# Edge-gated graph layer: early stores on another queue with rows taken earlier, low parts copied across partitions, expansion placed behind the aggregation

## Chip, cores and metric

One core of one Trainium2 chip. The metric is device time of one execution in microseconds. Each kernel runs several times in rounds beside the kernel before on the same chip. Chips differ by over 1% (the kernel before has medians of 1219 to 1235 us in four comparisons, three of them on chips known to differ), so only ratios are compared across chips. All runs told of here gave a correct result. Two timed runs were in the slow state (one of the kernel before at 1242.29 us, one of b_early_expand at 1246.37 us); the ratios leave them out. All profiles are of fast runs.

## The reference

```python
# x: [16, 1024, 256]; A_a = A_m = adj: [1024, 1024], about 1% non-zero
pre_u = einsum('bud,dk->buk', h, W1[:d]);  pre_v = einsum('bvd,dk->bvk', h, W1[d:])
hidden = relu(pre_u[:, :, None, :] + pre_v[:, None, :, :] + b1)
S = sigmoid(einsum('buvk,ko->buvo', hidden, W2)[..., 0] + b2[0])
a = einsum('buv,bud->bvd', S * A_a, h)
m = einsum('uv,bud->bvd', A_m, h) * h
z = beta1 * h + beta2 * (a @ Wa + ba) + beta3 * (m @ Wm + bm)
```

## The kernel before

The kernel works on lists of edges. An opening makes a table with, for each node u, its `pre_u` row (a product on TensorE) and its `h` row, and the edge lists of the first 512 targets v. Then 320 steps follow, 10 to a block (a block is 128 targets times 4 batches). A step takes 128 edges:

- GpSimd gathers the edges' table rows into one of five buffers `fetched`;
- TensorE **expands** `pre_v` from targets to edges with a 0/1 matrix `mark` (`expand`, into one of two buffers `pc`);
- VectorE adds both and reduces relu times W2 (`gate`); ScalarE takes the sigmoid and scales the left side;
- one step later TensorE **aggregates** (`aggregate`).

In between run the products of the block: `pre_v` of the next block (`halves`), table rows, the output of the last block, and the remaining edge lists. All of these share two small buffers, `misc`, in PSUM, the memory that products are written to. A product's result is copied out of PSUM by ScalarE or VectorE; this is called its eviction here. `pre_v` is kept as a rounded high part and a low part, stacked on the two halves of the partitions, so that one fp32r product carries both. The low part is made on its own partitions and has to get to the other half.

```python
# lists(vt): stages of one edge list; the masks of a list go to all partitions
few = ...; nc.scalar.copy(few, mark)
yield
for w in range(NW):
    for h in range(2):
        nc.scalar.dma_start(whose[h * W:(h + 1) * W, vt * NW + w, :], few[w * W:(w + 1) * W])
pe = aside(vt)
...                                                   # 5 products into pe
nc.scalar.copy(L..., pe...)
yield                                                 # VectorE goes on from L
...
# halves(k): pre_v of block k
for h in range(2):
    step = yield
    p = small("p"); add_row(p, b1_p); half_product(p, hTs[order[k]], w_v, h, True)
    nc.scalar.copy(X[:, 0, c], p)
    after(step + 1, lambda: nc.vector.tensor_tensor(low[:, c], p, X[:, 0, c].bitcast(FP), ALU.subtract))
yield
nc.scalar.copy(X[W:, 1, :], X[W:, 0, :].bitcast(FP))
for h in range(2):
    yield
    pl = small("pl")
    nc.tensor.matmul(pl, swap, low[:, c], start=True, stop=True)
    for w in range(NW):
        s = slice((1 - w) * W, (2 - w) * W)
        nc.scalar.copy(X[s, w, c], pl[s])
...
# the opening: digits advance a list by a stage, r is half a table row tile, h a stage of halves(0),
# v the small gathers of list 0's values, f the first five gathers
script = ("r 0 0", "r r 0", "r 1", "0 r 1 1", "0 0 r r", "1 r 0 2 2", "r 0 0 v 2", "1 1 r r 2",
          "r 1 r 3 3", "1 1 2 2 r h", "2 r r h 3", "2 2 3 h", "3 3 f h h")
...
for n in range(total + 2):                            # k, s: block and step in it
    aggregate(n - 1); fetch_val(2); fetch(n - 1 + NF) # and half_end twice a block
    gate(n); left_adj(n + 1)
    ...                                               # load_mark twice a block
    do(n)                                             # work put off with after()
    ...                                               # lists, block_end, turn_over
    if k + 1 < BS and s in (0, 2, 3, 4, 7): ...       # halves(k + 1)
    ...                                               # table rows
    if n + 2 < total:
        expand(n + 2)
```

Order matters: every engine takes its instructions in the order of the program.

## Time and profile before

| | kernel before |
|---|---|
| median of 3 runs, us | 1236.83 (1234.14 to 1241.36) |
| span of the profiled execution, us | 1225.1 |
| busy us: TensorE, VectorE, ScalarE, GpSimd | 1110.8, 1068.5, 844.0, 416.3 |
| add's (L546) idle ahead of it, us | 68.9, of it 38.9 for the expansion |
| first gather, first add, first add of the second block, us | 68.62, 78.14, 131.3 |

The profiled execution took 1226.9 us, less than any of the timed runs. Busy shares over the span mix an opening with no full engine and a loop with three nearly full ones, so they must be read by stage. The prediction below shows those views. Two groups matter later (columns: busy us, mean ns | idle us of the engine just ahead, with what ended it):

```profile
L546 DVE TENSOR_TENSOR t<-fetched,pc 128x1024 f32<-128x1024 f32 x320 | 389.2, 1216 | 68.9 <-PE pc L530 38.9 <-DMA fetched<-table,uidx 11.5 <-PE misc L385 4.8
L420 DVE TENSOR_TENSOR low<-misc,X 128x512 fp32r<-128x512 f32 x64 | 44.0, 687 | 20.6 <-ACT X L419 20.2 <-issue 0.3
```

### The profile page before, as it was taken

The numbers are of one execution on the slowest core, as the hardware profiler recorded it, in microseconds if no ns is written. First come the engines' busy times: TensorE is split into PE (matmuls) and PEld (weight loads), VectorE is DVE, ScalarE is ACT, GpSimd is POOL, SyncE is SP. The second block draws the span as 40 slices with busy tenths as digits, with TensorE's granted clock in tenths as the row PEclk, the third lists the DMA queues.
The fourth block names the chain that finished last, engine by engine and source line by source line (L and its number), as shares of the span: only waits on it lengthen the run. The fifth ranks groups of instructions, "written<-read, shape, count | busy, mean of one in ns | idle before, by whom it ended". The sixth has DMA issues, their size and how long they took to land. (4 is left out here: it accounts for less than half of the span.)

```text
span 1225.1 us, 23939 instructions
## 1 busy us (share of the span) xinstructions
PE 1110.8 (91%) x7697; PEld 723.6 (59%) x7697; DVE 1068.5 (87%) x3517; ACT 844.0 (69%) x2562; POOL 416.3 (34%) x412
## 2 busy tenths in 40 slices
PE   7665989988888988999999999999999999999986
PEld 6543666645555655666666556666666655665553
DVE  7667868898997889899999999998888999999994
ACT  2245567766666756778777777777777777887763
POOL 0345562326244314423233333332222333333330
PEclk9777999989898989999999999999999999999998
DMA  9688899977889979899999999999998998999992
GB/s 285 221 296 296 268 321 330 335 262 237 315 291 332 353 295 343 323 356 362 356 363 375 351 355 325 347 351 394 387 358 322 353 322 315 329 339 329 325 334 97
DMA packets 151975, 393.50 MB, mean 321 GB/s; under 512 B 16816, under 2 KB 110512, under 8 KB 115632
## 3 DMA queue, kind: packets, MB, share of 16 engines
q0 software_dynamic: 49504, 299.85, 66.5%
q1 hardware_dynamic: 85776, 77.08, 19.5%
q10 hardware_dynamic: 16560, 14.95, 3.8%
q8 instruction: 63, 1.03, 0.3%
q14 instruction: 72, 0.59, 0.1%
HBM read 395.88 MB, written 50.33 MB: 364 GB/s over the span
## 5 line engine op out<-in xcount | busy, mean ns | idle before, releaser
L459 POOL DMA_INDIRECT fetched<-table,uidx x320 | 326.7, 1021 | 717.1 <-PE acc L567 525.5
L550 DVE SCALAR_TENSOR_TENSOR t<-t,w_b 128x256 f32<-128x256 f32 x1280 | 469.6, 422 | 19.8
L546 DVE TENSOR_TENSOR t<-fetched,pc 128x1024 f32<-128x1024 f32 x320 | 389.2, 1216 | 68.9 <-PE pc L530 38.9
L567 PE MATMUL acc<-fetched,left 128*32 128x256 f32 x4096 | 323.4, 393 | 28.1 <-ACT left L556 21.9
L556 ACT ACTIVATE left<-left,gt 128x32 f32<-128x32 f32 (+1 forms) x1280 | 300.3, 306 | 10.4
L530 PE MATMUL pc<-X,mark 128*128 128x512 f32 x640 | 249.8, 472 | 5.4 <-ACT mark L523 5.4
L567 PEld LDWEIGHTS acc<-fetched,left 128*32 128x32 f32 x4096 | 121.3, 110 | 195.6 <-issue 71.6
L553 ACT ACTIVATE gt<-sc,b_b 128x4 f32<-128x4 f32 x320 | 95.5, 299 | 158.8 <-DVE t L550 150.7
L385 PE MATMUL misc<-w_u,hT 128*128 128x256 f32 x512 | 132.7, 407 | 19.8 <-ACT fetched L401 8.4
L530 PEld LDWEIGHTS pc<-X,mark 128*128 128x128 f32 x640 | 120.0, 195 | 29.8 <-ACT mark L523 5.9
L615 PE MATMUL misc<-w_m,LT 128*128 128x256 f32 x496 | 133.7, 392 | 0.0
L615 PE MATMUL misc<-w_a,LT 128*128 128x256 f32 x496 | 127.3, 379 | 0.0
L385 PEld LDWEIGHTS misc<-w_u,hT 128*128 128x128 f32 x512 | 99.3, 203 | 43.9 <-ACT fetched L401 8.9
L385 PE MATMUL misc<-w_v,hT 128*128 128x256 f32 x512 | 122.6, 383 | 0.0
L540 ACT ACTIVATE left<-onehot,val 128x128 f32<-128x128 bf16 (+1 forms) x320 | 117.5, 367 | 0.0
L615 PEld LDWEIGHTS misc<-w_m,LT 128*128 128x128 f32 x496 | 88.9, 189 | 34.8 <-issue 25.5
L385 PEld LDWEIGHTS misc<-w_v,hT 128*128 128x128 f32 x512 | 98.3, 192 | 13.2
L343 POOL DMA_INDIRECT val<-in_adjT_dram,vidx x80 | 85.3, 1066 | 60.9 <-DVE b_p L194 33.4
L550 DVE DVE_READ_ACCUMULATOR t<-t,w_b 128x1 f32 x1280 | 104.0, 81 | 0.0
L575 ACT COPY ev<-acc 128x512 f32<-128x512 f32 x128 | 74.9, 585 | 41.6 <-PE acc L567 28.6
L615 PEld LDWEIGHTS misc<-w_a,LT 128*128 128x128 f32 x496 | 94.2, 190 | 12.8
L585 PE MATMUL misc<-ident,ev 128*128 128x128 f32 x512 | 81.0, 289 | 15.8 <-DVE h_blk L619 8.5
(140 smaller groups left out, 820.3 us busy)
## 6 DMA issues: line engine op xcount, KB each, us to landing
hT<-in_xT_dram SPq DMA_DIRECT2D x40, 512.0 KB
h_blk<-in_x_dram SPq DMA_DIRECT2D x31, 512.0 KB
out_dram<-h_blk SPq DMA_DIRECT2D x31, 512.0 KB
table<-tab SPq DMA_DIRECT2D x26, 512.0 KB
table<-in_x_dram ACTq DMA_DIRECT2D x24, 512.0 KB
fetched<-table,uidx POOLq DMA_INDIRECT x320
table<-in_x_dram SPq DMA_DIRECT2D x8, 512.0 KB
table<-fetched SPq DMA_DIRECT2D x6, 512.0 KB
```

Of the source, the lines that this page charges most:

```text
L343: nc.gpsimd.indirect_dma_start(out=val[:, i, j:j + 1], out_offset=None, in_=adj_flat, in_offset=bass.IndirectOffsetOnAxis(ap=vidx[:, i, j: ...
L385: nc.tensor.matmul(p[:, bb * D:(bb + 1) * D], hT[:, 2 * h + bb, i, :], wt[:, i, :], start=(i == 0 and not begun), stop=(i == DC - 1), skip ...
L459: nc.gpsimd.indirect_dma_start(out=fetched[n % NF], out_offset=None, in_=table[g], in_offset=bass.IndirectOffsetOnAxis(ap=uidx[:, vt * NW ...
L530: nc.tensor.matmul(pcs[n][:, c], marks[n // TW][:, j * P:(j + 1) * P], cuts[k][:, w, c], start=True, stop=True)
L540: nc.scalar.activation(lefts[n][:, :m, :, 0, :], onehot[:, i, o:o + m, :].unsqueeze(2).to_broadcast([P, m, GB, V]), AF.Copy, scale=val[:, ...
L546: nc.vector.tensor_tensor(t, fetched[n % NF][:, :GD].rearrange("p (b d) -> p b d", b=GB), pcs.pop(n).rearrange("p (b d) -> p b d", b=GB), ...
L550: nc.vector.scalar_tensor_tensor(t[:, b, :], t[:, b, :], 0.0, w2_b, ALU.max, ALU.mult, accum_out=sc[:, b:b + 1])
L553: nc.scalar.activation(gt, sc, AF.Sigmoid, bias=b2_b)
L556: nc.scalar.activation(lefts[n][:, :m, b, 1, :], lefts[n][:, :m, b, 0, :], AF.Copy, scale=gt[:, b:b + 1])
L567: nc.tensor.matmul(accs[h][b * 2 * V:(b + 1) * 2 * V, r, :], left[:, i, b].rearrange("p k v -> p (k v)"), f[:, GD + b * D:GD + (b + 1) * D ...
L585: nc.tensor.transpose(pt[:, i * P:(i + 1) * P], ev[:, r, c * P:(c + 1) * P], ident)
L615: nc.tensor.matmul(pz[:, bb * D:(bb + 1) * D], LTs[k][:, c, 2 * h + bb, i, :], wt[:, c, :], start=False, stop=(i == 1 and c == DC - 1), sk ...
```

## The change

Its intent: free ScalarE's queue in the opening, have the table's rows done sooner, take the swap off TensorE, and give VectorE its expansion before TensorE turns to the block's products. There are three parts. Part 1 is the copies, part 2 the place of the expansion, part 3 the opening (stores and script). `EARLY` is 4, so lists 0 to 3 are meant. The cut is shortened.

```diff
-    swap = fixed([P, P], "swap", FR)                     # and its two instructions
-                nc.scalar.dma_start(whose[...], few[...])
+                (nc.gpsimd if vt < EARLY else nc.scalar).dma_start(whose[...], few[...])
@@ halves
-        for h in range(2):
+        for w in range(NW):
             yield
-            c = slice(2 * h * D, (2 * h + 2) * D)
-            pl = small("pl")
-            nc.tensor.matmul(pl, swap, low[:, c], start=True, stop=True)
-            for w in range(NW):
-                s = slice((1 - w) * W, (2 - w) * W)
-                nc.scalar.copy(X[s, w, c], pl[s])
+            nc.scalar.copy(X[(1 - w) * W:(2 - w) * W, w, :], low[w * W:(w + 1) * W].bitcast(FP))
@@ script
-    "r 0 0", "r r 0", "r 1", "0 r 1 1", "0 0 r r", "1 r 0 2 2", "r 0 0 v 2", "1 1 r r 2",
-    "r 1 r 3 3", "1 1 2 2 r h", "2 r r h 3", "2 2 3 h", "3 3 f h h"
+    "r 0 0", "r r 0", "r 1", "0 r 1 1", "0 0 r r", "1 r 0 2 2", "r r 0 0 v 2", "1 1 r r",
+    "2 r 1 r", "2 2 r r 1 1 h", "2 h 3 3", "2 2 h 3", "f h h 3", "3 3"
@@ main loop
         do(n)
+        if n + 2 < total:
+            expand(n + 2)
         ...
-        if k + 1 < BS and s in (0, 2, 3, 4, 7):
+        if k + 1 < BS and s in (0, 2, 3, 4, 6):
         ...
-        if n + 2 < total:
-            expand(n + 2)
```

More of the change, by code (lines that the diff above doesn't have):

```diff
@@ L178 @@
         nc.vector.tensor_scalar(slot_of[:, w, :], upto[:, :TW], float(P), row, ALU.mult, ALU.add)
-    swap = fixed([P, P], "swap", FR)
-    for w in range(NW):
-        nc.vector.tensor_scalar(swap[:, w * W:(w + 1) * W], upto[:, (1 - w) * W:(2 - w) * W], row, None, ALU.is_equal)
     ident = fixed([P, P], "ident")
@@ L305, in lists @@
             for h in range(2):
-                nc.scalar.dma_start(whose[h * W:(h + 1) * W, vt * NW + w, :], few[w * W:(w + 1) * W])
+                (nc.gpsimd if vt < EARLY else nc.scalar).dma_start(whose[h * W:(h + 1) * W, vt * NW + w, :], few[w * W:(w + 1) * W])
         pe = aside(vt)
@@ L423, in halves @@
         nc.scalar.copy(X[W:, 1, :], X[W:, 0, :].bitcast(FP))
-        for h in range(2):
+        for w in range(NW):
             yield
-            c = slice(2 * h * D, (2 * h + 2) * D)
-            pl = small("pl")
-            nc.tensor.matmul(pl, swap, low[:, c], start=True, stop=True)
-            for w in range(NW):
-                s = slice((1 - w) * W, (2 - w) * W)
-                nc.scalar.copy(X[s, w, c], pl[s])
+            nc.scalar.copy(X[(1 - w) * W:(2 - w) * W, w, :], low[w * W:(w + 1) * W].bitcast(FP))
     engines = mybir.EngineType
@@ L477 @@
         copy_h(turn[i], nc.sync)
-    script = ("r 0 0", "r r 0", "r 1", "0 r 1 1", "0 0 r r", "1 r 0 2 2", "r 0 0 v 2", "1 1 r r 2",
-              "r 1 r 3 3", "1 1 2 2 r h", "2 r r h 3", "2 2 3 h", "3 3 f h h")
+    script = ("r 0 0", "r r 0", "r 1", "0 r 1 1", "0 0 r r", "1 r 0 2 2", "r r 0 0 v 2", "1 1 r r",
+              "2 r 1 r", "2 2 r r 1 1 h", "2 h 3 3", "2 2 h 3", "f h h 3", "3 3")
     m = 0
```

## The prediction

> **What bounds the kernel now.** I read the row of tenths first, to see which engines are full where.
>
> ```profile
> PE   7665989988888988999999999999999999999986
> ...
> DVE  7667868898997889899999999998888999999994
> ...
> PEclk9777999989898989999999999999999999999998
> DMA  9688899977889979899999999999998998999992
> ```
>
> Three stages. The first three slices (about 78 us of 1225) have no engine full: an opening made of waits. Up to slice 16 (about 500 us) TensorE and VectorE share the work with gaps. From there on TensorE, VectorE and DMA all read 9. The table by stretches (us, then busy us and counts of PE, PEld, DVE, ACT, POOL, then clock, DMA share, GB/s) tells the last stage apart:
>
> ```profile
> 78.10:150.00 71.90, 55.65 (x330) 37.33 (x330) 55.63 (x189) 36.65 (x109) 38.28 (x37) 0.83 0.88 297
> 150.00:300.00 150.00, 137.09 (x911) 89.28 (x909) 126.64 (x419) 101.09 (x305) 61.66 (x61) 0.95 0.87 300
> 300.00:500.00 200.00, 176.79 (x1199) 112.35 (x1201) 175.88 (x584) 133.63 (x410) 77.66 (x76) 0.95 0.89 313
> 500.00:700.00 200.00, 195.56 (x1431) 127.28 (x1423) 186.62 (x599) 156.85 (x483) 63.17 (x63) 1.00 0.98 364
> ```
>
> From 500 us TensorE is busy 195.56 of 200 us (98%) and VectorE 186.62 (93%): TensorE is the bound, VectorE 5% behind. In 150 to 500 us TensorE has 36 us of gaps in 350. The chain that ended last covers only the final 22 us, so it says nothing here. The timeline of one late step shows the order on TensorE:
>
> ```profile
> 905.40 1.07 PE L567 MATMUL acc<-fetched,left 128*32 128x256 f32 x16
> 905.51 1.22 DVE L546 TENSOR_TENSOR t<-fetched,pc 128x1024 f32<-128x1024 f32 x1
> ...
> 908.05 0.58 PE L428 MATMUL misc<-low,swap 128*128 128x512 f32 x1
> ...
> 908.47 0.63 PE L530 MATMUL pc<-X,mark 128*128 128x512 f32 x2
> ...
> 909.13 1.22 DVE L546 TENSOR_TENSOR t<-fetched,pc 128x1024 f32<-128x1024 f32 x1
> ```
>
> A step on TensorE is aggregation (L567), products of the block, swap, expansion (L530). VectorE's add (L546) takes the expansion finished just before it. The swap holds TensorE for 908.47 - 908.05 = 0.42 us.
>
> For the opening I read the timeline from 27 us:
>
> ```profile
> 27.35 4.94 ACTq L306 DMA_DIRECT2D whose<-few  x4
> ...
> 32.34 0.40 ACT L313 COPY L<-pc 128x290 f32<-128x290 f32 x1 [4.46 <-PE misc L385]
> ...
> 32.77 0.18 DVE L317 TENSOR_TENSOR s_of<-slot_of,L 128x10 f32<-128x10 f32 x1 [5.35 <-ACT L L313]
> ...
> 34.31 3.53 PE L385 MATMUL misc<-w_u,hT 128*128 128x256 f32 x8 [2.48 <-ACT fetched L401]
> ```
>
> Four issues of list 0's stores sit on ScalarE's queue for 4.94 us. The copy behind them comes that late, and VectorE and TensorE wait for it. Whom the trace names as releaser of the copy (a matmul long over) is not the cause; the queue is. The same happens to list 1 (47.30, 2.64 us; VectorE idle 4.83) and list 3 (81.24 to 84.04). Nothing else is full then: DMA moves only 142 GB/s from 40 to 65 us. The first gather goes out at 68.62, when the last row of the table has landed, and the first add starts at 78.14.
>
> **What the Trainium skill says.** "DMA: Bandwidth & Descriptors", Issuing engines are not separate DMA queues: starting DMAs from another engine saves only the issuing sequencer's time. Agrees in kind: an issue of these stores has a median of 0.608 us on ScalarE, and that time is what the change moves. "PSUM — Partial Sum Buffer", Engine vs sequencer instructions: ScalarE, VectorE and GpSimd are strict FIFOs and matmuls go in program order. Agrees: the copy at 32.34. So order is worth time here. "TensorE: Matmul & The Clock Gate", Back-to-back issue gap: N/2.4 + 2.5 ns warm, 216 ns for 512 columns. The trace has 0.42 us for a swap, about twice; the trace decides. "ScalarE: Activation LUTs", What ACT_TABLE_LOAD costs: 186 ns + 0.833 ns per element with immediates, so 612 and 1039 ns for 512 and 1024 columns. The trace has 581 and 1045.
>
> **Part 1, low parts without TensorE.** Gone per block: two swaps on TensorE and four copies of 64x512 from PSUM on ScalarE. New: two copies of 64x1024 in SBUF across partitions. Their duration is that of the form already there (L423):
>
> ```profile
> L431 ACT CAST X<-misc 64x512 fp32r<-64x512 f32 x128 | 74.4, 581 | 24.7 <-PE misc L428 20.2 <-PE acc L567 0.8
> L428 PE MATMUL misc<-low,swap 128*128 128x512 f32 x64 | 36.4, 569 | 23.1 <-ACT LT L588 11.6 <-issue 6.8 <-DVE from L280 3.1
> L423 ACT CAST X<-X 64x1024 fp32r<-64x1024 f32 x32 | 33.4, 1045 | 0.4
> ```
>
> ScalarE: 128 x 0.581 = 74.4 us become 64 x 1.045 = 66.9, so 7.5 us less; ScalarE is at 78% late, so this is worth little by itself. TensorE: 64 x 0.42 = 27 us of occupation go, 42 of the 64 after 500 us (17.6 us) and 20 between 78 and 500 (8.4 us). The waits around them go as well. Swap on the buffer from ScalarE (LT L588) and the next product on ScalarE's eviction (X L431) make 5.7 + 4.9 us plus 1.4 of small ones after 500, and about 5.3 + 2.3 + 5.9 + 0.5 = 14 between 150 and 500. Some of the latter waits will reappear at the next instruction, as they are ScalarE's or VectorE's lateness and not the swap's. Sum on TensorE: 17.6 + 12.0 = 29.6 late, 22 early.
>
> **Part 2, expansion right behind the aggregation.** Nothing is added or removed. The expansion comes 0 to 2 us earlier, ahead of the block's products. It needs a buffer that the add two steps back frees: for the expansion at 908.47 that is the add at 902.65, done at 903.87, while its new place is behind the aggregation's 16 issues, about 906.4. So TensorE doesn't stall for it in a TensorE-bound step. VectorE's waits for it should mostly go (L546 on pc L530: 38.9 us in all, 12.8 of them in 150 to 500 and 13.2 after 500). As VectorE isn't the bound, this pays only by letting it run ahead of steps in which it has more work. I choose 5 us over the whole loop, an estimate from the 7.4 + 9.0 us that TensorE waits for the gated left side (L556), of which a third may go.
>
> **What part 1 is worth in time.** After 500 us VectorE has 650 us of work in 700. Taking 29.6 us away gives 670, VectorE at 97% and the DMA at 349 x 700/670 = 365 GB/s on average. Two engines both near full don't reach that; I take 60%: 18 us. In 78 to 500 I take half of 22: 11 us.
>
> **Part 3, the opening.** Stores of lists 0 to 3 move to GpSimd, which idles until 35.97 us. List 0 then gives back about 4.4 us (28.4 in place of 32.8 for the copy's reader), list 1 about 2.6, and the third and fourth some 2 together. Two rows come before list 2's matters, and list 3 moves two script lines later. That takes VectorE work of 1.2 + 1.65 us (L246, L253) away from in front of list 1, and should take part of TensorE's 3.7 us waits for an eviction. On the other side GpSimd gets about eight issues at 0.6 us, with 0.3 us gaps, between the ten small gathers (36 to 50 us) and the first large gather: by an estimate from the L240 issues of 0.58 to 0.65 us, 7 us, ending at about 54 us if the small gathers start 4 us earlier. So the first large gather can't come before 54 and may come at 56 to 58 in place of 68.6. The burst behind it (400 GB/s from 75 to 100 us) moves along but isn't shortened. I take 10 us.
>
> **Sum.** 18 + 11 + 5 + 10 = 44 us; I take off 5 us for what several estimates in a row leave out: 39. 1236.8 - 39 = 1198.
>
> **Rivals.**
> (a) VectorE or ScalarE becomes the bound. For: VectorE is at 95% after 1000 us, and the new copies wait on VectorE's low parts. Against: these are made a step or more before the copy's turn. Then part 1 gives a third, 10 + 5, and the total is about 1212.
> (b) DMA is already the bound after 500 us, its share being 0.98. For: VectorE waits 10.1 us there for gathers. Against: that is 13 times in some 190 steps, and stretches of 25 us reach 393 to 408 GB/s. Then the late 18 us shrink to 5 and the total is about 1211.
> (c) GpSimd's queue delays the first gathers, its stores waiting for ScalarE's masks in front of gathers. For: strict order. Against: it has idle time up to 36 us. Then the opening gives nothing: about 1208.
> (d) The expansion waits for the add and holds up the block's products. For: in VectorE-late steps the add starts only when the aggregation does. Against: the aggregation itself lasts 0.6 to 1.0 us of the add's 1.22. It costs up to 0.3 us in a third of 320 steps: 30 us, which would eat most of the gain and give about 1225.
>
> **Range and chances.** One of (a) to (c) gives 1208 to 1212, at the limit of 2% (1212.1); all parts in full, with the opening at 15 us, give about 1182. So 1183 to 1215. Faster by over 2%: 0.74; within 2%: 0.24; slower: 0.02, as no work is added to a full engine.
>
> **What would show it.** Right: no swap row; TensorE busy about 27 to 30 us less at the same clock or better; 64 more copies of 64x1024 at about 1.04 us; L546's wait on pc under 15 us; first gather near 57 and first add near 67 us; the list copy L313 within 1 us of its matmuls. Wrong: the stretches from 500 us as long as before with L546 waiting on gathers (rival b), L530 waiting on VectorE's L546 for over 20 us (d), or the first gather still at 65 or later with GpSimd's stores just ahead of it (c).

## The result and the profile after

Median 1201.80 us (1200.57 to 1209.87, 4 runs) against 1235.49 us (1232.73 to 1241.36, 4 runs). The ratio of the fast runs is 0.9737, 95% interval 0.9689 to 0.9785. A ratio here is the mean time of one kernel's fast runs over that of the other's of the same rounds, so not quite the ratio of the medians. The kernel is faster. Two later comparisons, on two chips, gave 0.9757 and 0.9758.

The profiled execution (span 1208.1 us) is the longest of the four, while that of the kernel before was a short one, so the two profiles are only 17.0 us apart and not 33. Near 840 us TensorE waited 8.7 us for one load of transposed rows there. In another execution (the run after_third below) the same row product waits 4.1 us, put down there to an add long over. The block that holds this product (21, counted from 0) takes from 34.5 to 46.3 us in the fourteen traces (37.7 before, 46.0 after), without a pattern by part, so one execution's total moves by up to 12 us with it. Where it matters I therefore compare by block and not by the end.

The row of tenths of the kernel after:

```profile
PE   7767899897789888999999999997999999999986
...
DVE  7769878997989997999999999996789999999994
...
PEclk9878999899989999999999999998999999999998
DMA  9998999878989987999999999999899999999992
```

The pit at slice 28 (TensorE 7, VectorE 6) is the load just told of. The table by stretches, with the columns of the prediction's:

```profile
78.00:150.00 72.00, 59.76 (x384) 38.78 (x383) 61.97 (x214) 42.33 (x122) 47.34 (x45) 0.95 0.93 301
150.00:300.00 150.00, 133.60 (x925) 87.66 (x925) 126.66 (x412) 103.18 (x307) 59.66 (x59) 0.97 0.86 301
300.00:500.00 200.00, 176.33 (x1214) 114.69 (x1210) 179.41 (x605) 135.10 (x405) 75.26 (x74) 0.97 0.91 323
500.00:700.00 200.00, 197.78 (x1441) 129.87 (x1440) 190.78 (x608) 159.51 (x485) 64.88 (x64) 1.00 0.98 365
```

From 500 us TensorE is fuller than before (197.78 of 200), although its swaps are gone, and VectorE is at 190.78. Both were brought closer to full; neither has 5% to spare.

The opening, from the timeline of the kernel after (start and length in us, engine, line, operation; in brackets the engine's idle time just ahead and what ended it, where `issue` means that the profile shows no wait):

```profile
24.80 2.10 POOL L303 DMA_DIRECT2D whose<-few  x4 [22.22 <-ACT few L297]
...
28.14 0.40 ACT L310 COPY L<-pc 128x290 f32<-128x290 f32 x1 [0.47 <-PE pc L306]
...
28.57 0.17 DVE L314 TENSOR_TENSOR s_of<-slot_of,L 128x10 f32<-128x10 f32 x1 [1.36 <-ACT L L310]
...
55.56 1.07 POOL L451 DMA_INDIRECT fetched<-table,uidx  x1 [4.63 <-DMA table<-tab]
...
66.92 0.72 ACT L297 CAST few<-made 128x640 uint8<-128x640 f32 x1 [7.02 <-DVE made L291]
67.55 0.72 ACT L515 CAST mark<-whose 128x640 fp32r<-128x640 uint8 x1
...
69.59 1.22 DVE L538 TENSOR_TENSOR t<-fetched,pc 128x1024 f32<-128x1024 f32 x1 [2.04 <-PE pc L522]
```

The four stores of list 0 take 2.10 us on GpSimd, beside everything else (in the other traces with ScalarE's stores, they hold ScalarE's queue for 2.89, 3.09 and 6.36 us, so the 4.94 us before is not a fixed cost). ScalarE's copy follows its products at once (28.14 in place of 32.34), and VectorE idles 1.36 in place of 5.35 us. The first gather is 13 us earlier. The first add is only 8.5 us earlier: its mask (67.55) stands on ScalarE behind a copy for list 3, which waited 7.02 us for VectorE.

The groups that answer to those of before:

```profile
L538 DVE TENSOR_TENSOR t<-fetched,pc 128x1024 f32<-128x1024 f32 x320 | 388.8, 1215 | 22.0 <-DMA fetched<-table,uidx 8.2 <-PE pc L522 3.2 <-PE misc L577 1.1
L522 PE MATMUL pc<-X,mark 128*128 128x512 f32 x640 | 237.3, 453 | 23.6 <-DVE t L538 17.4 <-ACT mark L515 5.0 <-issue 1.2
L417 DVE TENSOR_TENSOR low<-misc,X 128x512 fp32r<-128x512 f32 x64 | 43.9, 686 | 48.6 <-ACT X L416 46.9 <-issue 1.7
L423 ACT CAST X<-low 64x1024 fp32r<-64x1024 f32 x64 | 66.8, 1044 | 0.8
```

The add no longer waits for the expansion (3.2 in place of 38.9 us). In its place VectorE waits for the high part of `pre_v` (46.9 in place of 20.2 us, of which 12.2 belong to the late load), and TensorE's expansion waits 17.4 us for the add that frees its buffer.

Where the time went, from the times of the first add of a block (us): before 78.1, at block 1 131.3, at block 11 524.2; after 69.6, 114.7 and 506.6. So the lead is 8.5 us at the loop's start, 16.6 one block later and 17.6 at block 11. The last can't be trusted: in the changed kernel's two later traces block 11 starts at 508.5 and 491.5 us. From block 11 to 19 the median block takes 31.83 against 32.53 us, from 24 to 30 it takes 31.10 against 31.53.

The 8 us won inside block 0 are mostly one step. In the kernel before the add of step 9 came 12.9 us after that of step 8:

```profile
117.96 0.59 ACT L588 COPY LT<-misc 128x512 f32<-128x512 f32 x1 [2.54 <-remote]
118.60 1.11 PE L585 MATMUL misc<-ident,ev 128*128 128x128 f32 x4 [4.28 <-issue]
...
120.39 0.80 PE L428 MATMUL misc<-low,swap 128*128 128x512 f32 x1 [0.68 <-ACT LT L588]
...
122.45 3.78 PE L385 MATMUL misc<-w_u,hT 128*128 128x256 f32 x8 [1.26 <-ACT X L431]
...
126.77 1.22 DVE L546 TENSOR_TENSOR t<-fetched,pc 128x1024 f32<-128x1024 f32 x1 [5.71 <-PE pc L530]
```

At 112.77 us a small product for list 4 had taken one of the two `misc` buffers, and VectorE read it at 129.46 only. So transposes, swap and row product queue for the one that is left, each behind ScalarE's eviction of the last, and the expansion stands behind them all. Not all of the step is this queue: the first eviction (117.96) waited 2.54 us for something that the profile doesn't name (`remote`), b_opening and b_early_expand have 3.76 and 4.30 us of the same there, and the changed kernel has none on record (1.01 us in after_again). The same place in the kernel after:

```profile
103.80 0.73 PE L522 MATMUL pc<-X,mark 128*128 128x512 f32 x2 [0.95 <-issue]
...
107.62 1.12 PE L577 MATMUL misc<-ident,ev 128*128 128x128 f32 x4 [1.81 <-ACT left L532]
...
109.41 3.56 PE L382 MATMUL misc<-w_u,hT 128*128 128x256 f32 x8 [0.68 <-ACT LT L580]
...
110.00 1.21 DVE L538 TENSOR_TENSOR t<-fetched,pc 128x1024 f32<-128x1024 f32 x1
```

The queue is still there but shorter, and the expansion came ahead of it, so the add takes place beside it: 4.5 us for the step.

### The profile page after: what moved, and what is told of

It is laid out like the page before. It is cut to its first block, busy times and chain, and to the rows that moved or that the text cites. A ratio compares the mean times of both kernels' runs of the same rounds, so it can differ in the third digit from the quotient of the medians.

```text
span 1208.1 us, 23816 instructions
## 1 busy us (share of the span) xinstructions
PE 1095.2 (91%) x7633; PEld 721.5 (60%) x7633; DVE 1066.6 (88%) x3515; ACT 838.6 (69%) x2498; POOL 424.3 (35%) x428
## 5 line engine op out<-in xcount | busy, mean ns | idle before, releaser
L559 PE MATMUL acc<-fetched,left 128*32 128x256 f32 x4096 | 333.3, 394 | 36.9 <-ACT left L548 20.5
L522 PE MATMUL pc<-X,mark 128*128 128x512 f32 x640 | 237.3, 453 | 23.6 <-DVE t L538 17.4
L559 PEld LDWEIGHTS acc<-fetched,left 128*32 128x32 f32 x4096 | 128.7, 110 | 184.9 <-issue 51.4
L522 PEld LDWEIGHTS pc<-X,mark 128*128 128x128 f32 x640 | 97.2, 191 | 159.3 <-issue 107.6
L382 PE MATMUL misc<-w_u,hT 128*128 128x256 f32 x512 | 128.6, 400 | 25.7 <-DMA hT<-in_xT_dram 14.6
L607 PE MATMUL misc<-w_m,LT 128*128 128x256 f32 x496 | 127.1, 378 | 0.0
L607 PEld LDWEIGHTS misc<-w_m,LT 128*128 128x128 f32 x496 | 93.6, 189 | 17.3
L340 POOL DMA_INDIRECT val<-in_adjT_dram,vidx x80 | 84.7, 1058 | 34.1 <-issue 21.9
L417 DVE TENSOR_TENSOR low<-misc,X 128x512 fp32r<-128x512 f32 x64 | 43.9, 686 | 48.6 <-ACT X L416 46.9
```

The source lines that it names most:

```text
L340: nc.gpsimd.indirect_dma_start(out=val[:, i, j:j + 1], out_offset=None, in_=adj_flat, in_offset=bass.IndirectOffsetOnAxis(ap=vidx[:, i, j: ...
L382: nc.tensor.matmul(p[:, bb * D:(bb + 1) * D], hT[:, 2 * h + bb, i, :], wt[:, i, :], start=(i == 0 and not begun), stop=(i == DC - 1), skip ...
L522: nc.tensor.matmul(pcs[n][:, c], marks[n // TW][:, j * P:(j + 1) * P], cuts[k][:, w, c], start=True, stop=True)
L559: nc.tensor.matmul(accs[h][b * 2 * V:(b + 1) * 2 * V, r, :], left[:, i, b].rearrange("p k v -> p (k v)"), f[:, GD + b * D:GD + (b + 1) * D ...
L607: nc.tensor.matmul(pz[:, bb * D:(bb + 1) * D], LTs[k][:, c, 2 * h + bb, i, :], wt[:, c, :], start=False, stop=(i == 1 and c == DC - 1), sk ...
```

## The experiments

The question was which part gives how much, as the traces show gains in the opening, in block 0 and in the loop. **Theory S**: the loop's gain comes from the swaps being gone. **Rival E**: it comes from the earlier expansion. For the opening, **theory Q** (the stores on another queue) stood against **R** (the order of the rows). The first four runs undo one part of the changed kernel, the next four have one part alone (and the yardstick), the last four (with a yardstick too) look at the expansion again, at why the swap is worth less than its time on TensorE, and at list 3's copy. Each has a profile and five timed rounds; b_early_expand came to 22 runs.

| run | median us | before, us | ratio | 95% interval |
|---|---|---|---|---|
| a_swap_back | 1196.49 | 1220.50 | 0.9825 | 0.9794 to 0.9857 |
| a_late_expand | 1189.65 | 1220.50 | 0.9779 | 0.9742 to 0.9815 |
| a_act_stores | 1190.78 | 1220.50 | 0.9759 | 0.9736 to 0.9783 |
| a_old_script | 1189.59 | 1220.50 | 0.9739 | 0.9717 to 0.9760 |
| after_again | 1201.36 | 1231.98 | 0.9757 | 0.9722 to 0.9792 |
| b_no_swap | 1220.37 | 1231.98 | 0.9896 | 0.9867 to 0.9924 |
| b_early_expand | 1235.41 | 1231.98 | 1.0022 | 1.0001 to 1.0042 |
| b_opening | 1219.77 | 1231.98 | 0.9887 | 0.9851 to 0.9924 |
| after_third | 1188.69 | 1219.23 | 0.9758 | 0.9725 to 0.9792 |
| a_late_again | 1188.54 | 1219.23 | 0.9782 | 0.9738 to 0.9825 |
| c_dead_swap | 1187.74 | 1219.23 | 0.9775 | 0.9733 to 0.9816 |
| c_list3_later | 1184.95 | 1219.23 | 0.9722 | 0.9682 to 0.9762 |

Rows with the same time of the kernel before ran on the same chip. The changed kernel wasn't on the first chip, so its mates are held against 0.974 to 0.976.

### a_swap_back

```diff
-            nc.scalar.copy(X[(1 - w) * W:(2 - w) * W, w, :], low[w * W:(w + 1) * W].bitcast(FP))
+            pl = small("pl"); nc.tensor.matmul(pl, swap, low[:, c], start=True, stop=True)
+            for w in range(NW): nc.scalar.copy(X[s, w, c], pl[s])        # as before
```

> The changed kernel, but the low parts cross partitions by the two swaps on TensorE and four evictions per block again. Theory S (the gain in the loop comes from the swaps that are gone): the traces show the changed kernel gaining about 0.8 us per block from block 11 to 21, 0.3 per block in 1 to 10, 0.4 from 23 on, some 15 us in all; most of it should be lost here: about 1212 to 1216 us. Rival E (the gain in the loop comes from the earlier expansion, as VectorE no longer waits for it): at most 4 us lost, about 1205. The opening stays as in the changed kernel either way: second block's first add near 115 us.

Ratio 0.9825: about 0.7% or 8 us are lost. That lies between S and E, nearer to S. The median block from 11 to 19 is at 32.40 us and from 24 to 30 at 31.93, against 31.83 and 31.10; the second block's first add is at 114.6 us, as expected. So without the swaps the blocks of the loop are shorter, and the whole is worth some 8 us; by the intervals 4 to 14 us, so S's 12 isn't excluded. The three other variants on this chip have medians of 1189.6 to 1190.8 us, 6 to 7 below this one.

### a_late_expand and a_late_again

```diff
         do(n)
-        if n + 2 < total:
-            expand(n + 2)
         ...
+        if n + 2 < total:
+            expand(n + 2)
         if n == 100:
```

> The changed kernel, but the expansion is at the end of the step again. Theory S: 1 to 4 us lost, about 1204, VectorE's add waiting again some 30 us for the expansion without this setting the pace. Rival E: about 12 us lost, near 1214. A third possibility, that the early place costs more by TensorE waiting for the add (17.4 us in the changed kernel's trace) than it gives: it gets faster, about 1198.

> The changed kernel with the expansion at the end of the step, beside the changed kernel on one chip, as the first look (0.9779 with two long runs, against 0.9737 and 0.9757 elsewhere) doesn't settle it. If the early place pays only together with the rest (the blocks from 11 to 19 took a median of 31.83 us with it and 32.35 without, and 32.5 in the kernel before): 0.002 to 0.005 more than the changed kernel beside it. If it is worth nothing, or costs as in the kernel before (1.0022): the same or less.

0.9779 and 0.9782, both with intervals that overlap the changed kernel's. On the one chip that ran both, the medians are 1188.54 (late) and 1188.69 us (early). So E's 12 us fall: with the rest of the change in place the early expansion may be worth nothing. The ratios put it at some 3 us (0.0024 on the one chip, the low end of what was expected if it pays), the medians at none, and the intervals leave room for up to 8 us. The hint for it from the blocks 11 to 19 (32.35 us in the first run) didn't come back in the second (31.83).

VectorE's waits in the loop show what became of the wait. The changed kernel (after_third), from 70 to 1165 us, columns us in total, times, longest:

```profile
DVE low L417 <- ACT X L416: 28.7, 20, 7.4
...
DVE t L538 <- PE pc L522: 4.6, 4, 2.0
```

and with the late expansion (a_late_again):

```profile
DVE t L538 <- PE pc L522: 34.4, 21, 9.8
...
DVE low L417 <- ACT X L416: 6.4, 11, 1.2
```

The early expansion moves VectorE's wait from the add to the low part: `pre_v`'s product now comes behind the expansion, and the low part stands in VectorE's order where it stood. In steps 1, 11, 21 and 31 this can be seen as adds 6.2 to 6.7 us apart in after_third; a_late_again has no such step there, but has one of 8.2 us at step 8, where the kernel before has 12.9. The sums of the two waits are 33.3 and 40.8 us. The longest of each (7.4 and 9.8 us) is again at the row product with the late load; without it the sums are 25.9 and 31.0.

### a_act_stores and a_old_script

```diff
-                (nc.gpsimd if vt < EARLY else nc.scalar).dma_start(whose[...], few[...])
+                nc.scalar.dma_start(whose[...], few[...])                # a_act_stores
```

```diff
-    script = (..., "r r 0 0 v 2", "1 1 r r", "2 r 1 r", "2 2 r r 1 1 h", "2 h 3 3", "2 2 h 3", "f h h 3", "3 3")
+    script = (..., "r 0 0 v 2", "1 1 r r 2", ..., "2 2 3 h", "3 3 f h h")  # a_old_script, as before
```

> The changed kernel, but the stores of lists 0 to 3 are issued by ScalarE again. Theory Q (the 8 us at the first add and 17 us at the second block come from ScalarE's queue being free): list 0 loses 4.4 us, list 1 about 2.6, list 2 and 3 some 2 each: first gather 6 to 9 us later than 55.6, total about 1209. Rival R (the row order does it): at most 3 us lost, about 1204.

> The changed kernel, but with the opening's script of before. Theory Q: 3 to 5 us lost, about 1206, as VectorE's work for list 3 comes back in front of list 1's and ScalarE's mask copies in front of two evictions. Rival R: 8 us or more, about 1211. If both this and the stores alone lose the whole gain, the two only work together.

0.9759 and 0.9739 are no loss that these runs can see. The first fits R (at most 3 us lost) and not Q; for the second both theories expected too much. Yet the first gathers did move, to 60.70 and 61.35 us from 55.56. The first adds are at 75.6 and 70.7 us (69.6 in the changed kernel), those of the second block at 119.0 and 113.7 (114.7). So with the old script nothing is lost by then, and with ScalarE's stores some 4 us are, which the total doesn't resolve. Gathers that land earlier don't help where the first mask comes late (c_list3_later tests this). Undoing both halves of the opening at once wasn't run, so what the opening as a whole is worth in the changed kernel stays open.

### after_again and after_third

The changed kernel unaltered.

> The changed kernel unaltered, for a ratio with a narrow interval and for the three undone parts to be held against. Expected 0.972 to 0.975 of the kernel before, as on record; single runs 8 to 12 us longer than the rest may turn up, as in the profiled run on record, where TensorE waited 8.7 us for one load of transposed rows.

> The changed kernel once more, as the yardstick of this chip: 0.973 to 0.977 of the kernel before.

0.9757 and 0.9758, as on record. In after_third the row product that waits for the late load on record waits 4.1 us.

### b_no_swap, b_early_expand, b_opening

The kernel before with one part each. Their diffs are those parts of the change; b_no_swap has also step 6 in place of 7.

> The kernel before with the low parts copied across partitions, nothing else. Undoing this in the changed kernel cost some 0.9% (ratio 0.9825 against 0.974). Theory S: the same here, 0.990 to 0.992 (about 10 to 12 us). Rival E, in which the part only pays where the expansion is early: 0.996 or more.

> The kernel before with the expansion right behind the aggregation, nothing else. Undoing it in the changed kernel moved the ratio by about 0.003 within the noise. Theory S: 0.996 to 1.000. Rival E: 0.990 or less. VectorE's add should wait under 5 us for the expansion in place of 38.9, and TensorE some 20 us for the add in its place, which would show why it pays little.

> The kernel before with the new script and the stores on GpSimd, nothing else. If the opening's gain stands by itself, the second block's first add comes 13 to 17 us earlier than 131.3 and the ratio is about 0.987. Stores alone and script alone each left nearly all of the gain standing when the other was undone (0.976 and 0.974), so the two together need not be the sum of two parts. If the opening's gain is mostly the swap's absence in it (TensorE idle 3.07 us before the second swap), under 8 us, ratio 0.993.

The copies alone give 1.04% (13 us of 1232), the opening alone 1.13% (14 us), and the early expansion alone costs 0.22% (3 us, the interval just excludes zero). In b_early_expand the add's wait for the expansion falls to 8.8 us (under 5 expected), the low part's rises to 48.0, and TensorE waits 11.9 us for the add (some 20 expected). The parts sum to 24 us, the whole gives 30 (0.9757 on this chip). The traces show where they work together: at the second block's first add b_opening leads the kernel before by 8.4 us, b_no_swap by 2.7, b_early_expand is 3.0 late, and the changed kernel leads by 16.6. Step 8 of block 0 is 14.4 us in b_opening and 4.4 to 5.6 in the changed kernel's three profiles. Undoing only the swap or only the expansion leaves 114.6 and 113.1 us, so behind the new opening either of the two takes most of that hole away. Each of these leads is from a single execution, the trace of before from another comparison.

One trace doesn't fit the account of the swaps: in b_no_swap blocks 11 to 19 take a median of 33.70 us, more than the 32.53 before. Its blocks 24 to 30 do take 31.10, and its block 11 starts 10 us earlier than before (514.2 against 524.2). So the 13 us of the copies alone are shown by the time; where in the loop they arise, isn't.

### c_dead_swap

```diff
         for w in range(NW):
             yield
+            nc.tensor.matmul(small("pl"), swap, low[:, 2 * w * D:(2 * w + 2) * D], start=True, stop=True)
             nc.scalar.copy(X[(1 - w) * W:(2 - w) * W, w, :], low[w * W:(w + 1) * W].bitcast(FP))
```

> The changed kernel, with two swap products per block issued on TensorE again but read by nobody (the result is the same). It tells the 0.42 us that each holds TensorE from the chain swap, eviction, next product. Theory O (occupation): it costs nearly what the whole swap did, 0.006 to 0.009 in the ratio, some 8 to 11 us. Rival W (it was the waits for buffers and evictions around it): under 0.003, some 3 us. Blocks 11 to 19 should go back to about 32.4 us by O and stay at 31.9 by W.

0.9775 against 0.9758 and a median 1 us lower than the changed kernel's: not resolved from zero. The difference of 0.0017 is short of 0.006 to 0.009, but with an interval of about 0.005 to either side it doesn't quite exclude the low end. The 64 products are there, and hardly anything waits ahead of them:

```profile
L426 PE MATMUL misc<-low,swap 128*128 128x512 f32 x64 | 36.9, 576 | 1.6 <-DVE s_of L317 1.6
```

In the kernel before 23.1 us of idle time stood ahead of the same 64. But that is no sign of the chain, as in a_swap_back, with its evictions, it is only 1.5 us too. What a_swap_back has and this run hasn't is behind the swap:

```profile
L431 ACT CAST X<-misc 64x512 fp32r<-64x512 f32 x128 | 74.4, 581 | 40.4 <-PE misc L428 39.4
```

ScalarE stands idle for 39.4 us until the swaps' products are there, and the weights of the product behind wait 11.0 us for its evictions. Blocks 11 to 19 take 32.15 us (31.83 without, 32.40 with the whole swap), blocks 24 to 30 take 31.13 (31.10 and 31.93). The first lies about halfway, the second with the kernel without swaps. So the runs lean to W and against O, without settling it: a product that nobody evicts cost little here, on an engine that reads 98% busy. I infer that what the swap cost is mainly the chain buffer, product, eviction, next product. This is not shown: how much a wait of this chain alone costs wasn't run, and the 7.6 us that ScalarE's evictions take beyond the copies (74.4 against 66.8) weren't told apart from it.

### c_list3_later

```diff
-              ..., "f h h 3", "3 3")
+              ..., "f h h 3")
-    advance = {0: (3,), 2: (3,), 4: (3,)}
+    advance = {0: (3,), 1: (3,), 2: (3,), 4: (3,), 5: (3,)}
```

> The changed kernel with two stages of list 3 moved from the opening's end into steps 0 and 1. In the changed kernel ScalarE's first mask sat 7.0 us behind list 3's copy, and the first gather 5 us earlier than with the old script gave no time. If that copy sets the start of the loop: first add at 62 to 65 us in place of 69, and 3 to 6 us gained (ratio 0.003 to 0.005 less than the changed kernel). If the burst of gathers behind the opening sets it (DMA share 1.05 from 65 to 78 us): the first add comes earlier, but the second block's stays near 114 us and the time too.

The first add comes at 63.95 us and the second block's at 109.7 (71.1 and 114.2 in after_third beside it):

```profile
58.60 0.72 ACT L515 CAST mark<-whose 128x640 fp32r<-128x640 uint8 x1
...
63.95 1.22 DVE L538 TENSOR_TENSOR t<-fetched,pc 128x1024 f32<-128x1024 f32 x1 [3.74 <-DMA fetched<-table,uidx]
```

The mask is 9 us earlier than in the profile on record (10.5 than in after_third), and the add now waits for its gather. So list 3's copy did set the start of the loop. The total is 3.7 us lower (1184.95 against 1188.69) with overlapping intervals, the fastest kernel of this study but not shown to be faster than the changed one.

## Why the prediction was right

The forecast of 1198 us and of a gain over 2% held (1201.80; 0.9737): 39 us were forecast and 33.7 measured. Its terms held less well than their sum, and that the sum came out near is in part luck.

- **Part 3, the opening, taken as 10 us:** right in mechanism, somewhat small. Alone it gave 14 us. List 0 gave back 4.2 us as worked out, and the first gather came at 55.6 us (56 to 58 named). Not foreseen: the first add hung on list 3's copy on ScalarE and not on the gather, and the opening's lead grew in block 0 together with the other parts.
- **Part 1, the swaps, taken as 18 + 11 us:** right in sign, two to three times too large. It gave 13 us alone and some 8 as the last part. The step that failed is "64 x 0.42 = 27 us of occupation go": put back as occupation alone, in c_dead_swap, they show no loss that can be told from zero. TensorE's busy time fell by 15.6 us only, where 27 to 30 were named, while the rows of other products grew (aggregation 323.4 to 333.3 us for the same 4096); as ends of matmuls are modelled, a reading of 98% may hold slack that no view shows. The waits around the swap, which the working had next to it (12.0 us late, 14 early), are what the runs point to, without showing it.
- **Part 2, the expansion, taken as 5 us:** not borne out. Alone it is 3 us slower. The step that failed is that a third of TensorE's waits for the gated left side would go: that wait was 21.9 us before and is 20.5 after (26.5 in after_third). What was foreseen is that VectorE's own wait doesn't set the pace; that it would come back at the low part wasn't.
- **The 5 us taken off, and luck:** the parts measured alone give 13 + 14 - 3 = 24 us where 44 were summed. The 5 us taken off make up for a quarter of this. The rest of what brought the forecast near is that the parts together gave 6 us more than their sum (30), for which the prediction has no term.
- **Readings and sums:** "Nothing else is full then" holds for 40 to 65 us, but while list 0's stores were issued the DMA share was 1.09 (28 to 32 us, 339 GB/s). The steps after 500 us are 218 and not "some 190", and VectorE's row reads 8 in slices 28 to 31, not 9. The lower end of 1182 us doesn't follow from the terms: 49 us as taken, with 15 for the opening, give 1188; with TensorE's sums in full (29.6 + 22) it is 1165. In rival (a) 5 us are less than the third of 22 that is named.

Of the rivals, (a) is partly there: in blocks 24 to 30 the changed kernel, both runs with a late expansion, c_dead_swap and b_no_swap all have a median of 31.1 to 31.2 us, with VectorE at 192 of 200 us in after_third from 920 us, so less work on TensorE hardly shows there (b_opening, with its swaps, is at 31.13 in its one trace, but a_swap_back at 31.93, so this isn't the whole of it). (b) isn't seen: the add's waits for gathers went from 11.5 to 8.2 us (11.1 in after_third). (c) isn't either: GpSimd's last stores in front of the first gather were done 4.6 us ahead of it. (d) is there in part: TensorE waits 17.4 us for the add, just under the 20 us that I had named as the limit (20.3 in after_third), and b_early_expand is slower.

Open stays whether the early expansion is worth anything in the changed kernel, by which way the swap cost its 8 to 13 us, and what the wait for the late load near 840 us, which differs between executions, hangs on.

## What to carry to other kernels

A busy engine's row doesn't say what a piece of its work is worth: put the piece back without its consumers and see, before giving it a price by its duration. Where a product and its eviction share a few small buffers with others, look at the chain around it too: in block 0 one step took 12.9 us with one of two buffers held by another tile. When an order is changed to end a wait, look what else stood behind the old place: here the wait moved from one VectorE instruction to the next, and the time didn't.

## What the Trainium skill lacked or had wrong

- "DMA: Bandwidth & Descriptors", Issuing engines are not separate DMA queues: it calls the issuing time usually small beside the DMA itself; the section gives no figure. Here one store of 40 KB holds ScalarE's queue for 0.608 us and GpSimd's for 0.540 us in the median. List 0's four held ScalarE's for 4.94 us (2.89 to 6.36 in other traces) and GpSimd's for 2.10 us, and VectorE idled 5.35 us behind the first.
- "TensorE: Matmul & The Clock Gate", Back-to-back issue gap: its N/2.4 + 2.5 ns, the gap of an isolated product, is 216 ns for 512 columns, and it has less for a stream. The fp32r products here followed each other at 0.42 us in the median; the section doesn't speak of fp32r.
- "ScalarE: Activation LUTs", What ACT_TABLE_LOAD costs: the formula held for 1024 columns (1039 ns against 1044 measured) and was 5% high for 512 out of PSUM (612 against 581), but the section doesn't say whether a copy to other partitions costs more. It didn't here: a median of 1044 ns for 64x1024 across the halves, 1042 ns in place.
